# Loads of a three-layer attention kernel reordered around its first attentions, and one masked q moved to ScalarE

## The chip, the cores and the metric

The kernel runs on one core of one Trainium2 chip. The metric is device time in microseconds of the whole program. The core has five engines that run side by side, each with its own instruction stream in a fixed order: TensorE (PE in the profile; its weight loads are PEld), VectorE (DVE), ScalarE (ACT), GpSimd (POOL) and SyncE (SP). SP and ACT issue the transfers (DMAs) between memory and the on-chip SBUF; matmuls write to PSUM.

## The reference

There are 16 batches of 256 tokens with 256 features, a stream x and a context y. Three attentions and an MLP follow one another per batch, each attention with 16 heads of 16 features:

- layer 0: q from rmsnorm(x)·g_q, k and v from rmsnorm(y)·g_c; softmax over the unmasked keys; output projection, added to x, and another rmsnorm with g_out;
- layer 1: layernorm, causal self-attention with rotary position terms on q and k, biases, output projection, residual;
- layer 2: layernorm for q, k and v from y itself, rotary terms, no mask, output projection, residual;
- MLP: layernorm, 256 to 1024, tanh-gelu, 1024 to 256, residual.

All is float32. Layernorm's gain is folded into the weights in the kernel (w = g·w), and its bias into the projection biases (b·w, a product of a vector and a weight matrix).

## The kernel before, in words

`ORDER` (line 31) lists 48 attentions; digit i is the layer of attention i, and equal digits take the batches in turn. The first five are of layer 0, the first of layer 1 is i=5, the first of layer 2 is i=11. After them comes the MLP, two batches at a time.

One attention works in feature-major tiles. `q` and `k` (`by_feature`, L290) and `v` (`by_token`, L303) are projections of 16 matmuls into a PSUM tile d of 512 columns, of pool psD (three buffers). `scores(n)` computes block n of the score matrix, transposed, into two tiles S of 1024 columns (pool psS has two), and ScalarE takes each through exp into pt (L483). A causal attention has three blocks, with a GpSimd select (L490) that zeroes what lies above the diagonal; the others have four. `values(n)` multiplies pt with v into A (L511, one buffer in psA). A row of ones in v gives the sums of the softmax. `take` copies A to av and stores it to a scratch tensor hop in memory; `end` reads the sums and the rotated output oT back; `invert` takes the reciprocal and spreads it over another scratch trip; `divide` and `project` finish.

The masked q: heads are paired, and `qm` holds q twice, once with the odd heads zeroed and once with the even ones. For layers 1 and 2 `rotated` (L393) makes ScalarE add the bias, VectorE swap halves (a shuffle), multiply by the cosine and sine tables and add; then two VectorE operations (L424) write the two masked copies. k goes the same way without the masking.

The work is written out by hand in a loop over i and n (from line 879): block n of attention i stands beside q (n=0), k (n=1) and v (the last but one) of attention i+1, the output projection of i-2, and the statistics and norms of i+2. The order on every engine is the written one, and so is the order of the DMAs on SP's queue. There an entry waits for its data and holds up all that follow it; each of the DMAs also waits for an earlier one to land, since eight semaphores are used in turn.

Before the loop all starting loads are issued (L93 to L125): vec, the three weights of layer 0 and its output weight on ACT's queue, x, xT (x transposed), yT, y and the mask on SP's. For attention 0 `spread` brings the row scale of x across the partitions with a matmul against `ident`. For later ones of layer 0 `send` and `receive` do it through memory (rq).

Weights of later layers come inside the loop from SP's queue: sa (layer 1) before i=0, ca (layer 2) and fc1 at i=0, sao, cao and fc2 at i=1. `fold_bias` at i=1, n=3 forms the products b·w of sa, ca and fc1 on TensorE (L185), stores them to memory and reads them back transposed in the next entry of the queue (L196); `fold_cols` uses them at i=3. `fold_v` forms the one for v of layer 1. `fold_gain` (L226) is g·w. Two `idle` matmuls (L167) run before the first data.

Of the kernel before, what the change touches and what calls it, by code (L numbers as in the profile page):

```python
# [15 lines left out]
P = 128  # L16
# [29 lines left out]
def xattn_kernel(  # L46
# [45 lines left out]
    def load_x(b):  # L92
        nc.sync.dma_start(out=rows_of(b), in_=x[b].rearrange("(c p) d -> p c d", p=P))  # L93
        xTs[b] = work.tile([P, KC, S], F32, tag="xT", name=f"xT{b}", bufs=3)
        nc.sync.dma_start(out=xTs[b], in_=xt[b].rearrange("(k p) s -> p k s", p=P))

# [16 lines left out]

    vec = ctile([P, NVEC + 2], "vec")
    nc.scalar.dma_start(out=vec, in_=vecs)
    load_x(0)
    w0_sb = ctile([P, KC, 3 * D], "w0")
    load_w(w0_sb, w0, nc.scalar)
    load_y(0)
    mask_u8 = ctile([P, B * NC], "mask_u8", U8)  # L120
    nc.sync.dma_start(out=mask_u8, in_=mask)
    load(1)
    w0o_sb = ctile([P, KC, D], "w0o")
    load_w(w0o_sb, [w0_o], nc.scalar)
    load(2)  # L125
# [39 lines left out]
    idle = dense_ps()  # L165
    for n in range(2):
        nc.tensor.matmul(  # L167
            idle, lhsT=ident, rhs=zeros, start=True, stop=True
        )

# [4 lines left out]
    def fold_bias():  # L175

        ps = dense_ps()
        sets = (
            [(sa_sb, 0, V_B1), (sa_sb, D, V_B1), (ca_sb, 0, V_B2), (ca_sb, 0, V_B2)],
            [(fc1_sb, j * D, V_B3) for j in range(4)],  # L180
        )
        for n, items in enumerate(sets):
            for k in range(KC):
                for j, (w, at, vcol) in enumerate(items):
# [3 lines left out]
                        rhs=w[:, k, at : at + D],  # L188
# [3 lines left out]
        nc.scalar.copy(sb, ps)  # L192
        hop = dram.tile([4, 2 * D], F32, tag="fold", name="fold_hop", bufs=1)
        nc.sync.dma_start(out=hop, in_=sb[0:P:32])
        cols = ctile([P, 4, 2, KC], "cols")
# [6 lines left out]
    def fold_cols(cols):  # L202
        qk = vec[:, V_QK : V_QK + 8].rearrange("p (n t) -> p n t", t=KC)
        nc.vector.tensor_tensor(qk_bias[:, 0:3], cols[:, 0:3, 0], qk[:, 0:3], ALU.add)
        nc.vector.tensor_copy(qk_bias[:, 3], qk[:, 3])
# [18 lines left out]
    def fold_gain(w, cols, vcol, chunks=range(KC)):  # L224
        for k in chunks:
            nc.vector.tensor_scalar(  # L226
# [57 lines left out]
    def by_feature(src, w, at):  # L284

        ps = dense_ps()
        for t in range(KC):
# [23 lines left out]
    class Att:  # L311
# [36 lines left out]
        def spread(self):  # L348

            self.rq = work.tile([P, S], F32, tag="rq", name="rq")  # L350
            ps = dense_ps()
# [59 lines left out]
        def q(self):  # L411
# [11 lines left out]
            for i in range(2):  # L423
                nc.vector.tensor_scalar(self.qm[:, :, i, :], a, parity[i], None, ALU.mult)  # L424
# [437 lines left out]
    with tc.manual_schedule():  # L862
        do(0, "stats_x")
        fold_gain(w0_sb, slice(0, D), V_GQ)
        fold_gain(w0_sb, slice(D, 2 * D), V_GC)
        do(0, "turn", "spread", "q", "k", "stats_y")
# [12 lines left out]
        for i in range(N_ATT):  # L879
# [12 lines left out]
            for n in range(len(a.blocks)):  # L892
# [8 lines left out]
                if n == 0:  # L901
# [22 lines left out]
                    do(i + 1, "q")  # L924
# [31 lines left out]
                if i == 0 and n == 1:  # L956
                    load_w(ca_sb, ca, nc.sync)
                if i == 0 and n == 2:
                    load_w(fc1_sb, [fc1], nc.sync)
                if i == 1 and n == 0:  # L960
                    load_w(sao_sb, [sa_o], nc.sync)
                    load_w(cao_sb, [ca_o], nc.sync)
                if i == 1 and n == 2:
                    load_w(fc2_sb, [fc2], nc.sync)
# [504 lines left out]
```

## Time and profile before

| what | us |
|---|---|
| median of 3 runs (lowest, highest) | 946.64 (946.43, 946.78) |
| the profiled execution's own time | 946.89 |
| its span, first to last instruction | 945.2 |
| PE busy | 931.8 |
| DVE busy | 665.9 |
| ACT busy | 546.8 |
| POOL busy | 305.6 |
| mean granted TensorE clock, share of full | 0.997 |
| HBM read, written | 50.92 MB, 30.17 MB |

In lines of a profile the name before `<-` is what is written, the names after it what is read; x and a number count instructions; the last bracket gives the idle time before the group and what ended it. A line of the chain gives start, length and what ran. A line of a stretch gives its bounds and length, then busy time and instruction count of PE, PEld, DVE, ACT and POOL, then the granted clock, the DMA share and GB/s. DMAs are busiest in the first 26 us, at about 330 GB/s; over the span they move 86 GB/s.

### The profile page before, as it was taken

How to read it: one execution, taken by the hardware profiler on the slowest of the kernel's cores; microseconds unless marked ns; L12 is line 12 of the kernel's file. 1: busy time of each engine (PE TensorE's matmuls, PEld its weight loads, DVE VectorE, ACT ScalarE, POOL GpSimd, SP SyncE). 2: the span in 40 equal slices, each digit the busy share in tenths (PEclk: the TensorE clock that was granted, in tenths of full speed). 3: DMA queues.
4: the chain of work that ended last, by engine and by line, in shares of the span. 5: the costliest groups of instructions: out<-in, count | busy, mean ns of one | idle time of the engine just before them, and what ended most of it. 6: DMA issues, size and time to landing. Idle time of an engine off the chain costs nothing.

```text
span 945.2 us, 29295 instructions
## 1 busy us (share of the span) xinstructions
PE 931.8 (99%) x12374; PEld 549.6 (58%) x12374; DVE 665.9 (70%) x1438; ACT 546.8 (58%) x770; POOL 305.6 (32%) x501
## 2 busy tenths in 40 slices
PE   8999999999999999999999999999999999999997
PEld 3444555445454555455454454455444799999997
DVE  4346777787777787768876667998877576666663
ACT  3656656666666666756656666666666634444440
POOL 4122543324253464243343333454133021222200
PEclk9999999999999999999999999999999999999999
DMA  9543442323232233222343221222222100000001
GB/s 304 192 133 109 136 132 71 122 77 121 82 116 87 67 125 107 91 87 62 125 127 126 81 91 59 79 74 81 65 75 79 42 23 24 12 12 24 24 24 48
DMA packets 97955, 83.06 MB, mean 88 GB/s; under 512 B 21524, under 2 KB 97300, under 8 KB 97816
## 3 DMA queue, kind: packets, MB, share of 16 engines
q1 hardware_dynamic: 96584, 80.05, 26.7%
q8 instruction: 99, 1.62, 0.7%
q10 hardware_dynamic: 1232, 1.07, 0.3%
q14 instruction: 40, 0.33, 0.1%
HBM read 50.92 MB, written 30.17 MB: 86 GB/s over the span
## 4 chain that ended last, share of the span: by engine, by line
PE 95%; DMA 2%; DVE 1%; POOL 0%; ACT 0%; SPq 0%; issue 0%; ACTq 0%; DVEq 0%
PE S L472 19%; PE A L511 18%; PE d L303 17%; PE d L290 17%; PE upX L676 6%; PE A L774 5%; PE downZ L774 3%; PE upZ L676 3%; PE d L270 2%; PE d L774 2%; PE d L676 1%; PE d L652 1%; PE downX L774 1%; DMA w<-in_w_Wk 1%; DMA fold_hop<-fold 1%; DMA hop<-av 0%
## 5 line engine op out<-in xcount | busy, mean ns | idle before, releaser
L483 ACT ACTIVATE pt<-S 128x1024 f32<-128x1024 f32 x224 | 217.3, 1022 | 122.3 <-PE S L472 122.3
L472 PE MATMUL S<-qm,kT 32*128 32x512 f32 (+1 forms) x1536 | 201.9, 600 | 2.3 <-ACT hT L275 1.4
L511 PE MATMUL A<-pt,va 128*32 128x256 f32 (+1 forms) x3072 | 189.6, 368 | 2.3 <-DVE av L528 2.3
L511 PEld LDWEIGHTS A<-pt,va 128*32 128x32 f32 x3072 | 80.3, 109 | 156.0 <-issue 100.3
L483 ACT ACTIVATE pt<-S,sy 128x1024 f32<-128x1024 f32 x128 | 135.7, 1111 | 47.3 <-PE S L472 46.7
L490 POOL TENSOR_SCALAR_AFFINE_SELECT pt<-pt 128x512 f32<-128x512 f32 x128 | 89.5, 716 | 61.0 <-ACT pt L483 60.5
L472 PEld LDWEIGHTS S<-qm,kT 32*128 32x128 f32 x1536 | 62.1, 183 | 68.1 <-issue 39.9
L234 POOL TENSOR_SCALAR r_ln<-bmv 128x2 f32<-128x2 f32 x48 | 13.8, 287 | 222.5 <-DVE bmv L253 221.3
L279 POOL TENSOR_TENSOR cur<-cur,bias 128x512 f32<-128x512 f32 x48 | 66.7, 1395 | 56.5 <-DVE xn L259 56.5
L398 ACT ACTIVATE a<-d,qk_bias 128x256 f32<-128x256 f32 x128 | 53.8, 471 | 51.2 <-PE d L290 41.3
L290 PE MATMUL d<-hT,sa 128*32 128x256 f32 x1024 | 61.1, 379 | 0.0
L571 DVE TENSOR_TENSOR cur<-d,cur 128x512 f32<-128x512 f32 x32 | 22.0, 687 | 50.1 <-PE d L303 50.1
L406 DVE TENSOR_TENSOR u<-u,turn 128x512 f32<-128x512 f32 x64 | 53.9, 843 | 0.0
L528 DVE COPY av<-A 128x512 f32<-128x512 f32 x47 | 32.4, 689 | 26.9 <-PE A L511 26.9
L259 DVE TENSOR_SCALAR xn<-cur,bmv,r_ln 128x256 f32<-128x256 f32 x96 | 50.7, 577 | 0.8 <-POOL r_ln L235 0.3
L406 DVE TENSOR_TENSOR a<-a,turn 128x512 f32<-128x512 f32 x64 | 47.0, 735 | 2.2
L402 DVE STREAM_SHUFFLE u<-a 128x512 f32<-128x512 f32 x64 | 47.6, 743 | 0.0
L714 ACT ACTIVATE g<-g,fb 128x256 f32<-128x256 f32 x96 | 41.0, 499 | 11.1 <-DVE g L703 11.1
L290 PEld LDWEIGHTS d<-hT,sa 128*32 128x32 f32 x1024 | 33.2, 110 | 22.0
L234 POOL TENSOR_SCALAR r_o<-ms_o 128x2 f32<-128x2 f32 x16 | 4.7, 294 | 126.8 <-DVE sq L242 116.4
L562 DVE TENSOR_TENSOR oT<-oT,inv 128x512 f32<-128x512 f32 x48 | 42.7, 889 | 1.9 <-DMA inv<-inv_hop 1.9
L769 DVE TENSOR_TENSOR g<-g,g 128x512 f32<-128x512 f32 x64 | 40.9, 682 | 0.0
(149 smaller groups left out, 1560.7 us busy)
## 6 DMA issues: line engine op xcount, KB each, us to landing
hop<-av SPq DMA_DIRECT2D x96, 256.0 KB
oT<-hop SPq DMA_DIRECT2D x96, 128.0 KB
inv<-inv_hop SPq DMA_DIRECT2D x96, 128.0 KB
cur<-in_x SPq DMA_DIRECT2D x16, 256.0 KB
xT<-in_xt SPq DMA_DIRECT2D x16, 256.0 KB
yT<-in_yt SPq DMA_DIRECT2D x16, 256.0 KB
y<-in_y SPq DMA_DIRECT2D x16, 256.0 KB
out<-res SPq DMA_DIRECT2D x15, 256.0 KB
```

Of the source, the lines that this page charges most:

```text
L259: nc.vector.tensor_scalar(xn[:, c, :], src[:, c, :], mv[:, c, 0:1], r[:, c : c + 1], ALU.subtract, ALU.mult,)
L279: nc.gpsimd.tensor_tensor(t, t, bias_sb[:, row : row + D].unsqueeze(1).to_broadcast([P, NC, D]), ALU.add)
L290: nc.tensor.matmul(ps[j : j + 32, t * S : (t + 1) * S], lhsT=w[:, k, at + t * P + j : at + t * P + j + 32], rhs=src[:, k, :], start=(k == ...
L303: nc.tensor.matmul(ps[j : j + 32, c * D : (c + 1) * D], lhsT=src[:, k, c * P + j : c * P + j + 32], rhs=w[:, k, at : at + D], start=(k == ...
L398: nc.scalar.activation(a[:, t], ps[:, t], AF.Identity, bias=bias[:, t : t + 1])
L406: nc.vector.tensor_tensor(t, t, table.unsqueeze(1).to_broadcast([P, KC, S]), ALU.mult)
L472: nc.tensor.matmul(ps[:, j, 2 * m * u : 2 * m * (u + 1)] .rearrange("p (i s) -> p i s", i=2), lhsT=self.kT[r, t, kc * P : (kc + 1) * P], r ...
L483: nc.scalar.activation(pt[:, :, :w], ps[:, :, :w], AF.Exp, scale=scale)
L490: nc.gpsimd.affine_select(out=diag, in_=diag, compare_op=ALU.is_ge, fill=0.0, base=0, pattern=[[0, 2], [0, 2], [1, P]], channel_multiplier=-1,
L511: nc.tensor.matmul(self.av[32 * r : 32 * r + 32, i, q0:S], lhsT=self.va[:, kc, 8 * t + 2 * r + i, :], rhs=pts[r // 2][:, r % 2, i * m : (i ...
L676: nc.tensor.matmul(banks[c // 2][:, (c % 2) * S : (c % 2 + 1) * S], lhsT=a[:, c * P : (c + 1) * P], rhs=b, start=(first and c % 2 == 0), s ...
L774: nc.tensor.matmul(ps[:, c, :], lhsT=a[f // 2][:, f % 2, c * P : (c + 1) * P], rhs=b[:, f, :], start=(first and c == 0 and f == 0), stop=True,
```

## The change

- **Loads.** Only vec, Wq and Wk (on ACT) and xT, x, yT, y of batch 0 (on SP, xT now ahead of x) are issued first. The rest of the starting loads stand on SP behind a `gate`: a one-word store that reads Wq after its gain is folded in. Wv and Wo move from ACT's queue to SP's.
- **Later weights.** ca moves to i=3, cao and fc1 to i=4, fc2 to i=6.
- **Folds.** `fold_bias` is split: for sa at i=1 (8 matmuls, the two products twice over), for ca and fc1 at i=6 (16). The read-back is a function of its own, at i=2 and i=8. `fold_v` moves to i=0, n=3. The gain of fc1 goes from VectorE at i=6 and 10 to GpSimd at i=10 and 12, and the combining steps of the MLP's weights start after i=12 instead of i=10.
- **First attention.** q is computed before `spread`; k in two halves with a copy each; `stats_y` between; the masked q in four pieces. Wq's gain comes first on VectorE, ahead of the statistics of x. `spread` uses psA's tile, the idle matmuls psS's and are 512 and 256 wide.
- **Masked q.** Where attention i is causal and i+1 is of layer 1 or 2 (i = 21, 28, 38, 40, 42), the second masked copy is an ACTIVATE on ScalarE, written right after the q that it belongs to.

```diff
     def load_x(b):
-        nc.sync.dma_start(out=rows_of(b), in_=x[b].rearrange("(c p) d -> p c d", p=P))
         xTs[b] = work.tile([P, KC, S], F32, tag="xT", name=f"xT{b}", bufs=3)
         nc.sync.dma_start(out=xTs[b], in_=xt[b].rearrange("(k p) s -> p k s", p=P))
+        nc.sync.dma_start(out=rows_of(b), in_=x[b].rearrange("(c p) d -> p c d", p=P))
...
+    w0_sb = ctile([P, KC, 3 * D], "w0")
+    load_w(w0_sb[:, :, : 2 * D], w0[:2], nc.scalar)
     load_x(0)
-    w0_sb = ctile([P, KC, 3 * D], "w0")
-    load_w(w0_sb, w0, nc.scalar)
     load_y(0)
     mask_u8 = ctile([P, B * NC], "mask_u8", U8)
-    nc.sync.dma_start(out=mask_u8, in_=mask)
-    load(1)
     w0o_sb = ctile([P, KC, D], "w0o")
-    load_w(w0o_sb, [w0_o], nc.scalar)
-    load(2)
...
-    def fold_bias():
+    def fold_bias(sets):
...
-        nc.scalar.copy(sb, ps)
-        hop = dram.tile([4, 2 * D], F32, tag="fold", name="fold_hop", bufs=1)
-        nc.sync.dma_start(out=hop, in_=sb[0:P:32])
-        cols = ctile([P, 4, 2, KC], "cols")
+        nc.scalar.copy(sb[:, :w], ps[:, :w])
+        hop = dram.tile([4, w], F32, tag=f"fold{len(sets)}", name="fold_hop", bufs=1)
+        nc.sync.dma_start(out=hop, in_=sb[0:P:32, :w])
+        return hop
+
+    def fold_back(hop):
...
-    def q(self):
+    def q(self, shared=False):
...
-            for i in range(2):
-                nc.vector.tensor_scalar(self.qm[:, :, i, :], a, parity[i], None, ALU.mult)
+            nc.vector.tensor_scalar(self.qm[:, :, 0, :], a, parity[0], None, ALU.mult)
+            if shared:
+                nc.scalar.activation(self.qm[:, :, 1, :], a, AF.Copy, scale=parity[1])
+            else:
+                nc.vector.tensor_scalar(self.qm[:, :, 1, :], a, parity[1], None, ALU.mult)
+
+        def first_qk(self):
+            self.qm = work.tile([P, KC, 2, S], F32, tag="qm", name="qm", bufs=2)
+            self.kT = work.tile([P, KC, S], F32, tag="kT", name="kT", bufs=2)
+            ps = by_feature(self.hT, self.w, 0)
+            self.spread()
+            for t in range(KC):
+                nc.scalar.copy(self.kT[:, t], by_feature(self.kvT, self.w, D, [t])[:, t])
+            self.stats_y()
+            for t in range(KC):
+                for i in range(2):
+                    nc.vector.scalar_tensor_tensor(
+                        self.qm[:, t, i, :], ps[:, t], parity[i], self.rq, ALU.mult, ALU.mult
+                    )
...
+        idle = psS.tile([P, 2, 512], F32, tag="S", name="idle")[:, 0]
+        for n in (512, 256):
+            nc.tensor.matmul(idle[:, :n], lhsT=ident, rhs=zeros[:, :n], start=True, stop=True)
+        fold_gain(w0_sb, slice(0, D), V_GQ)
+
+        gate = dram.tile([1, 1], F32, tag="gate", name="gate", bufs=1)
+        nc.sync.dma_start(out=gate, in_=w0_sb[0:1, KC - 1, 0:1])
+        load_w(w0_sb[:, :, 2 * D :], w0[2:], nc.sync)
+        nc.sync.dma_start(out=mask_u8, in_=mask)
+        load(1)
+        load_w(w0o_sb, [w0_o], nc.sync)
+        load(2)
         do(0, "stats_x")
-        fold_gain(w0_sb, slice(0, D), V_GQ)
         fold_gain(w0_sb, slice(D, 2 * D), V_GC)
-        do(0, "turn", "spread", "q", "k", "stats_y")
+        do(0, "turn", "first_qk")
...
-                    do(i + 1, "q")
+                    if i + 1 < N_ATT:
+                        att(i + 1).q(shared=a.causal)
...
-                if i == 0 and n == 1:
-                    load_w(ca_sb, ca, nc.sync)
-                if i == 0 and n == 2:
-                    load_w(fc1_sb, [fc1], nc.sync)
+                if i == 0 and n == 3:
+                    fold_v()
                 if i == 1 and n == 0:
                     load_w(sao_sb, [sa_o], nc.sync)
-                    load_w(cao_sb, [ca_o], nc.sync)
                 if i == 1 and n == 2:
-                    load_w(fc2_sb, [fc2], nc.sync)
...
                 if i == 1 and n == 3:
-                    cols = fold_bias()
-                    fold_v()
+                    sa_hop = fold_bias([[(sa_sb, 0, V_B1), (sa_sb, D, V_B1)] * 2])
+                if i == 2 and n == 2:
+                    sa_cols = fold_back(sa_hop)
...
+                if i == 3 and n == 2:
+                    load_w(ca_sb, ca, nc.sync)
                 if i == 3 and n == 3:
-                    fold_cols(cols)
+                    fold_sa(sa_cols)
+                if i == 4 and n == 2:
+                    load_w(cao_sb, [ca_o], nc.sync)
+                    load_w(fc1_sb, [fc1], nc.sync)
+                if i == 6 and n == 2:
+                    load_w(fc2_sb, [fc2], nc.sync)
+                if i == 6 and n == 3:
+                    ca_hop = fold_bias(
+                        [[(ca_sb, 0, V_B2)] * 4, [(fc1_sb, j * D, V_B3) for j in range(4)]]
+                    )
+                if i == 8 and n == 2:
+                    ca_cols = fold_back(ca_hop)
                 if i == 8 and n == 3:
                     fold_gain(ca_sb, slice(0, D), V_G2)
-                if i in (6, 10) and n == 3:
-                    fold_gain(fc1_sb, slice(0, FF), V_G3, [i // 10])
-                if n == 1 and i > 10 and not a.causal:
+                    fold_ca_fc1(ca_cols)
+                if i in (10, 12) and n == 1:
+                    fold_gain(fc1_sb, slice(0, FF), V_G3, [i // 12], nc.gpsimd)
+                if n == 1 and i > 12 and not a.causal:
```

More of the change, by code (lines that the diff above doesn't have):

```diff
@@ L163, in xattn_kernel @@
     nc.gpsimd.memset(zeros, 0.0)
[L165 to L169, printed above, removed]
     qk_bias = ctile([P, 4, KC], "qk_bias")
     fb1 = ctile([P, FF // P], "fb1")
-    def fold_bias():
+    def fold_bias(sets):
         ps = dense_ps()
[L178 to L181, printed above, removed]
+        w = len(sets) * D
         for n, items in enumerate(sets):
             for k in range(KC):
-                for j, (w, at, vcol) in enumerate(items):
+                for j, (t, at, vcol) in enumerate(items):
                     nc.tensor.matmul(
@@ L187, in fold_bias @@
                         lhsT=vec[:, vcol + k : vcol + k + 1].to_broadcast([P, 32]),
-                        rhs=w[:, k, at : at + D],
+                        rhs=t[:, k, at : at + D],
                         start=(k == 0), stop=(k == KC - 1), skip_group_check=True,
@@ L191, in fold_bias @@
         sb = work.tile([P, 2 * D], F32, tag="a", name="fold")
-        nc.scalar.copy(sb, ps)
-        hop = dram.tile([4, 2 * D], F32, tag="fold", name="fold_hop", bufs=1)
-        nc.sync.dma_start(out=hop, in_=sb[0:P:32])
-        cols = ctile([P, 4, 2, KC], "cols")
+        nc.scalar.copy(sb[:, :w], ps[:, :w])
[3 more added lines that the diff above has]
+    def fold_back(hop):
+        w = hop.shape[1]
+        cols = ctile([P, 4, w // D, KC], f"cols{w // D}")
         nc.sync.dma_start(
@@ L200, in fold_bias, with fold_sa, fold_ca_fc1 @@
         return cols
[L202 to L205, printed above, removed]
+    qk_cols = vec[:, V_QK : V_QK + 8].rearrange("p (n t) -> p n t", t=KC)
+    def fold_sa(cols):
+        nc.vector.tensor_tensor(qk_bias[:, 0:2], cols[:, 0:2, 0], qk_cols[:, 0:2], ALU.add)
+    def fold_ca_fc1(cols):
+        nc.vector.tensor_tensor(qk_bias[:, 2], cols[:, 0, 0], qk_cols[:, 2], ALU.add)
+        nc.vector.tensor_copy(qk_bias[:, 3], qk_cols[:, 3])
         nc.vector.tensor_tensor(
@@ L222, in fold_v, with fold_gain @@
         nc.vector.tensor_tensor(row, ps[:, :D], row, ALU.add)
-    def fold_gain(w, cols, vcol, chunks=range(KC)):
+    def fold_gain(w, cols, vcol, chunks=range(KC), eng=nc.vector):
         for k in chunks:
-            nc.vector.tensor_scalar(
+            eng.tensor_scalar(
                 w[:, k, cols], w[:, k, cols], vec[:, vcol + k : vcol + k + 1], None, ALU.mult
@@ L281, in add_bias, with by_feature @@
         )
-    def by_feature(src, w, at):
+    def by_feature(src, w, at, ts=range(KC)):
         ps = dense_ps()
-        for t in range(KC):
+        for t in ts:
             for k in range(KC):
@@ L350, in spread @@
             self.rq = work.tile([P, S], F32, tag="rq", name="rq")
-            ps = dense_ps()
+            ps = psA.tile([P, 2, S], F32, tag="A", name="A").rearrange("p i s -> p (i s)")
             for c in range(NC):
```

## The prediction

> **What bounds the kernel now.** A score step is one block's S matmuls (L472) to the next block's. I read the busy totals first, then the chain of work that ended last between 22 and 72 us, a table of stretches, and the timeline where TensorE (PE) is not fed.
>
> ```profile
> PE 931.8 (99%) x12374; PEld 549.6 (58%) x12374; DVE 665.9 (70%) x1438; ACT 546.8 (58%) x770; POOL 305.6 (32%) x501
> ```
>
> PE is the bound: time goes away only where PE idles, runs at a lowered clock, or has fewer matmuls. Its idle places: the start, 64 to 67 us, two gaps of 0.69 us at 345 and 449, and the last store. The chain names the second:
>
> ```profile
> 49.70 6.40 DMA fold_hop<-fold
> ...
> 56.57 3.55 DMA hop<-av
> ...
> 60.14 1.94 DMA sums<-hop
> ...
> 66.96 1.93 PE A L511 x16
> ```
>
> The SyncE (SP) queue is in order. The read-back of the bias fold (L196) sits in it behind its own write, so hop, sums, and with them VectorE (DVE), come late; the copy of av that frees A (L528) ends at 66.8.
>
> ```profile
> 64.00:67.00 3.00, 0.69 (x12) 0.07 (x6) 2.92 (x9) 2.12 (x2) 1.46 (x2) 0.92 0.15 48
> 67.00:71.00 4.00, 4.00 (x48) 2.04 (x48) 3.26 (x9) 0.00 (x0) 1.86 (x4) 0.64 0.70 224
> ```
>
> PE does 0.69 of 3 us, then runs at clock 0.64. Scores start at 63.51 and next at 71.12, against the usual 3.80 (32.26, 36.06, 39.86): 3.81 us lost.
>
> ```profile
> 8.51 0.62 DVE L226 TENSOR_SCALAR w<-w,vec 128x256 f32<-128x256 f32 x2 [2.60 <-DMA w<-in_w_Wk]
> 11.60 1.14 PE L472 MATMUL S<-qm,kT 32*128 32x512 f32 x8 [0.69 <-ACT kT L433]
> 15.17 0.64 PE L354 MATMUL d<-ident,pad 128*32 128x128 f32 x16 [0.57 <-POOL pad L235]
> 27.47 2.13 PE L472 MATMUL S<-qm,kT 32*128 32x512 f32 x8 [0.26 <-ACT pt L483]
> 589.18 1.95 ACT L483 ACTIVATE pt<-S 128x1024 f32<-128x1024 f32 x2 [0.26 <-PE S L472]
> 591.51 1.01 DVE L422 TENSOR_TENSOR a<-a,u 128x512 f32<-128x512 f32 x1
> 596.36 1.01 DVE L431 TENSOR_TENSOR kT<-a,u 128x512 f32<-128x512 f32 x1
> 597.51 1.14 PE L472 MATMUL S<-qm,kT 32*128 32x512 f32 x8
> 345.75 1.14 PE L472 MATMUL S<-qm,kT 32*128 32x512 f32 x8 [0.69 <-ACT hT L275]
> ```
>
> The start waits for Wk (8.5). In the causal attention of 588 the next k is ready at 597.4, 0.1 before its scores: no slack. At 345 the same chain is 0.69 late.
>
> [...] the trace's 2.31 us gap already gave 0.64[...] Here every ACT row does follow the order written. [...] the rotary multiply takes 0.69 us alone and 1.12 beside a select. [...]
>
> **The change part by part.**
>
> Start. Ahead of the gate stand six loads of 256 KB and vec, 1.6 MB. At the trace's 330 GB/s from 2.0 us they end near 7, so Wk comes at 7.0 to 7.5. But first_qk changes what ends last. DVE scales Wq first (Wq came at 5.2, two by 0.35, to 5.9), and only then takes the sums of squares of x (1.0, to 6.9); POOL's pad (1.15) is ready at 8.1; spread on PE 0.65, ACT's rq 0.4: 9.2. PE is in order: q, spread, k half 0, k half 1 (0.87 each): 10.5. On DVE the Wk gain (0.62) and stats_y (1.0) fit before 9.2, two qm pieces by about 0.4 give 10.0. So scores start at 10.5 instead of 11.60: -1.1 (bounds -0.6, -1.6). The wait for the second pad (0.57 at 15.17) shrinks with it: DVE finishes qm at 10.9, Wv gain 11.5, cast, x(1) 12.7, pad 13.8; spread at 13.9 against 15.17: another -0.2.
> The gate itself is a one-word store; SP behind it waits until 5.9. Behind it queue Wv (issued 6.5, needed 11.5), mask, load(1), w0o, load(2). Their issue was already held by earlier landings (L99 waited until 8.50 for Wk), and load(1)'s y landed at 13.66; now about 12. Later loads slip by the DMA gap, about 0.8 us: bias and turn, which drained at 26.3, come near 27. DVE's add in fold_v waits for that; next behind it on DVE is the av copy, needed near 29. Hidden.
>
> Fold matmuls. Before: 16 + 8 instructions between scores at 39.86 and 44.52, 24 by 0.108 = 2.6 plus drain, 2.91 in all. After: fold_v at i=0 (8), the sa fold at i=1 (8), the ca and fc1 fold at i=6 (16). With 8, a scores-to-scores step is 1.07 + 0.67 + 1.19 = 2.93. At i=0 the step was 29.53 - 26.14 = 3.39 from values to values, 1.66 of it a wait for ACT's exp, which fold_v now fills: -0.45. At i=1, 4.66 becomes 2.93: -1.73. At i=6, +1.73. Sum -0.45.
>
> SP stall. The read-back now stands at i=2, n=2, a step or more after its write; ca comes at i=3, cao and fc1 at i=4, fc2 at i=6, each two score steps before the next hop (7.6 us against at most 2.4 MB, 7 us). The 3.81 us go; bounds -2.3 (the idle alone) and -3.8.
>
> Masked q on ScalarE. It is shared only where the running attention is causal and the next is not layer 0: i = 21, 28, 38, 40, 42, five times. DVE loses one of two operations of 0.76 (0.44 without POOL). But on ACT the copy stands between q's bias ACTIVATEs and the next two exps, and waits for DVE's add. At i=38, from the scores at 587.95: bias ends +1.0, DVE's shuffle 0.74 and three operations by 0.69 (POOL has nothing to select now) end +3.8; copy to +4.5 (0.7). The exps, at +1.2 before, run +4.5 to +6.4; then k's bias ACTIVATEs +6.4 to +7.2 (were +3.9 to +4.8). Queued behind: POOL's selects, then values at +7.1 (was +6.6), project, turn: PE is ready for the next scores at +10.1 (was +9.56). DVE's chain for k starts at +7.25: 2.8 us if alone, +10.1; if it meets the selects, now pushed beside it, 3.4, +10.7. So the scores come 0.6 to 1.2 late, I take 0.9; at 21 and 28, where 0.69 is lost already, -0.1 to +0.5, I take 0.25. Sum 3 x 0.9 + 2 x 0.25 = +3.2 (bounds +1.6, +4.6).
>
> The rest at nothing: the fc1 gain moves to POOL at i=10 and 12 (1024 wide, at most two by 1.74 of L627's), into idle stretches of about 9 us before the next r_o; without that cover up to 3 us twice. The combine steps start two attentions later and still end long before the MLP. 2 x 512 idle columns become 768, before the first load lands. x and xT swap, inside the start.
>
> Sum: -1.3 - 0.45 - 3.81 + 3.2 = -2.4. The profiled execution took 946.89 (span 945.2, 1.7 around it), the median is 946.64; the step applies to both: **944.3 us**. A difference under 0.2%, 1.9 us, is about what a measurement here cannot tell from none.
>
> **The rivals.**
> The copy is hidden: if exps have room, the five cost nothing and the two gaps of 0.69 go: -5.6 - 1.4 = -7, 939.7. For it: ACT is busy 58%, less in causal attentions. Against: k's chain ends 0.1 us before its scores.
> Contention: kT at the late bound, +4.6, and fold_v waiting for sa, which lands near 24 if everything slips (needed 25.4), +0.5: -0.5, 946.1, no change.
> The stall stays: if hop or sums are late for other reasons, DVE is still blocked near 62: -1.3 - 0.45 + 3.2 = +1.4, 948.1, also near no change. For it: hop to sums took 6.7 us at 31.39; against: ca and fc1 filled the DMAs then, and are gone.
> Slower: the held exps. It decides from (5.55 + 1.9)/5 = 1.5 us a time. The price would be met if DVE reaches q's add later, each 1 us of delay before it holding exp, select, values and k alike: at 1.8 us, +9 - 5.6 = +3.4, 950.1. Against: in all five places DVE had sat idle 0.23 to 0.67 us when q's bias released it, so nothing is queued ahead of that chain.
>
> **How the numbers follow.** Forecast 0.38 (its own range 942 to 944.7); hidden copy 0.16; contention 0.22; stall stays 0.10; slower 0.14. Faster 0.54, same 0.32, slower 0.14. The range for 8 in 10 runs from near the hidden copy, 940.3, to 947.8, leaving out half of the slower case and a little below.
>
> **What would show it.** First scores near 10.5 and no PE gap or lowered clock between 55 and 70; the fold's read-back without its 6 us wait; fold matmuls at three places; in the five causal attentions exp starting 3 us later behind the copy and the next scores 0.6 to 1.2 late. Wrong if those exps are not held, if PE waits for fold_v's operands near 25, or if idle PE lowers the clock there or in the start.

## The result and the profile after

The changed kernel takes 954.37 us in the median (953.02 to 957.98, six executions) beside 946.71 for the kernel before on the same chip: ratio 1.0079, 95% interval 1.0058 to 1.0101. The forecast was 944.3, the range 940.3 to 947.8. The profiled execution took 953.12 us, its span is 951.4 against 945.2.

First the busy totals of the changed kernel, then three of TensorE's waits in it (engine and line, what ended the wait: us in total, times, longest), two of the kernel before, and three stretches of the changed kernel: the two where the kernel before had stood still (0.69 of 3 us busy) and run at a granted clock of 0.64, and a new one.

```profile
PE 936.0 (98%) x12390; PEld 551.9 (58%) x12390; DVE 663.8 (70%) x1434; ACT 548.8 (58%) x777; POOL 306.9 (32%) x503
```

```profile
PE d L267 <- DVE xn L256: 3.0, 2, 2.3
PE S L488 <- DVE kT L447: 2.9, 5, 0.6
...
PE A L527 <- DVE av L544: 1.0, 1, 1.0
```

```profile
PE A L511 <- DVE av L528: 2.3, 1, 2.3
...
PE S L472 <- ACT hT L275: 1.4, 2, 0.7
```

```profile
64.00:67.00 3.00, 3.00 (x48) 1.31 (x44) 1.04 (x4) 1.91 (x4) 0.54 (x3) 1.00 0.12 15
67.00:71.00 4.00, 4.00 (x68) 1.89 (x62) 1.56 (x5) 2.79 (x5) 0.00 (x0) 1.00 0.28 88
100.75:103.00 2.25, 0.10 (x4) 0.00 (x0) 0.81 (x4) 0.31 (x1) 0.54 (x1) 1.00 0.19 47
```

The old hole is gone: PE is busy in every microsecond from 64 to 71. The kernel before waited once for av, in that hole, and twice 0.7 us for hT. The changed kernel waits for xn (two places, 2.3 and 0.7), for kT (the five places of the masked q) and for av in another place.

To see what each is worth, take the start of every score step (attention i, step n) in both profiles and subtract. The difference changes in a few places only, and between them it is constant to some hundredths:

| at (i, n) | what | difference changes by, us | prediction |
|---|---|---|---|
| (0, 1) | start | -1.34 | -1.3 |
| (1, 0) to (2, 1) | fold_v moved, sa fold alone | -1.27 | -2.18 |
| (3, 2) | stall at 64 us | -3.81 | -3.81 |
| (6, 0) | wait for xn | +2.33 | 0 |
| (7, 0) | ca and fc1 fold | +1.73 | +1.73 |
| (8, 0) | wait for xn | +0.81 | 0 |
| (9, 2) | wait for av | +1.06 | 0 |
| 22, 29 | masked q on ScalarE | +0.85, +0.86 | +0.25 each |
| 39, 41, 43 | masked q on ScalarE | +1.53, +1.54, +1.52 | +0.9 each |
| after (47, 0) | MLP part | +0.4 | 0 |

The sum is +5.8 at (47, 0) and +6.2 in the span. The last +0.4 belongs to this one execution: from (47, 0) on the other kernels with the same MLP part take 225.5 to 225.8 us, the kernel before 225.5, this profile 225.9. All that was expected to be gained was gained but for 0.9 us of the folds, in this execution; then 4.2 us were lost in attentions 5 to 9 and 6.3 in the five places of the masked q.

The first loss, from the profile of SyncE's queue (start, length, what was issued), in the changed kernel and then, around the same hop, in the kernel before:

```profile
87.69 0.38 SPq L545 DMA_DIRECT2D hop<-av  x1
88.12 0.46 SPq L111 DMA_DIRECT2D cao<-in_ca_wo  x1
88.64 0.49 SPq L111 DMA_DIRECT2D fc<-in_fc  x1
89.17 0.52 SPq L94 DMA_DIRECT2D xT<-in_xt  x1
...
93.62 0.89 SPq L545 DMA_DIRECT2D hop<-av  x1
100.20 0.55 SPq L552 DMA_DIRECT2D sums<-hop  x1
```

```profile
97.96 0.37 SPq L529 DMA_DIRECT2D hop<-av  x1
102.24 0.55 SPq L536 DMA_DIRECT2D sums<-hop  x1
```

cao and fc1 (1.25 MB) are written for step 2 of attention 4, which starts at 80.48. SyncE comes to them at 88.1, when attention 5 has begun, and right behind them stands the 1 MB of inputs for a later attention. The second half of the hop goes out at 93.62 and has landed at 100.20, when the read of the sums can go: 6.6 us, against 4.3 in the kernel before. Then the chain runs through VectorE (start, length, what ran):

```profile
100.20 1.93 DMA sums<-hop
102.13 0.02 issue
102.15 0.19 DVE sums L563
102.34 0.02 issue
102.37 0.35 DVE sums L564
102.72 0.24 DVE xn L256
```

VectorE had waited 7.5 us for the sums, and xn, which TensorE turns next, is queued behind them. At (8, 0) it is fc2 in place of fc1 (the hop takes 6.11 us), and ahead of (9, 2) VectorE waits 0.87 us for the read-back of the second fold, which takes 5.55 us for 8 KB in single words; the copy of av that frees A stands behind it. From the same chain:

```profile
124.79 6.11 DMA hop<-av
130.97 1.96 DMA sums<-hop
...
148.37 5.55 DMA cols<-fold_hop
```

The second loss, in the order of time around the q of attention 39 (i=38), in the changed kernel. The scores before it started at 589.17; in the kernel before, all this stood against 587.95.

```profile
593.07 0.73 ACT L422 ACTIVATE qm<-a,vec 128x512 f32<-128x512 f32 x1 [2.92 <-DVE a L419]
...
593.70 1.91 ACT L499 ACTIVATE pt<-S 128x1024 f32<-128x1024 f32 x2
...
594.75 2.04 PE L488 MATMUL S<-qm,kT 32*128 32x512 f32 x8
...
595.51 0.83 ACT L395 ACTIVATE a<-d,qk_bias 128x256 f32<-128x256 f32 x2
...
597.17 0.87 DVE L403 TENSOR_TENSOR a<-a,turn 128x512 f32<-128x512 f32 x1
597.96 1.12 DVE L403 TENSOR_TENSOR u<-u,turn 128x512 f32<-128x512 f32 x1
...
599.12 1.01 DVE L447 TENSOR_TENSOR kT<-a,u 128x512 f32<-128x512 f32 x1
...
600.27 1.14 PE L488 MATMUL S<-qm,kT 32*128 32x512 f32 x8 [0.58 <-DVE kT L447]
```

ScalarE waits 2.92 us for VectorE's add, copies, and only then runs the two exps, +4.5 after the scores instead of +1.2. The next scores (594.75) take 2.04 instead of 1.14: their second tile S has to wait until a held exp has emptied it (its weight loads wait 0.61 us for that exp). k's bias follows at +6.3, and VectorE's chain for k now runs beside GpSimd's pushed-back selects (595.68 to 599.58): its multiplies and its add take 0.87, 1.12 and 1.01 us, where those for q at 590.96, with no select beside them, took 0.69, 0.68 and 0.69. From shuffle to the end of kT it is 3.75 us. The scores of attention 39 start 0.90 + 0.58 = 1.48 late.

### The profile page after: what moved, and what is told of

Read it like the earlier page. It is cut to its first block, busy times and chain, and to the rows that moved or that the text cites. A ratio compares the mean times of both kernels' runs of the same rounds, so it can differ in the third digit from the quotient of the medians.

```text
span 951.4 us, 29306 instructions
## 1 busy us (share of the span) xinstructions
PE 936.0 (98%) x12390; PEld 551.9 (58%) x12390; DVE 663.8 (70%) x1434; ACT 548.8 (58%) x777; POOL 306.9 (32%) x503
## 4 chain that ended last, share of the span: by engine, by line
PE 88%; DVE 5%; DMA 3%; ACT 2%; issue 1%; SPq 1%; POOL 0%; ACTq 0%; DVEq 0%
PE S L488 18%; PE A L527 17%; PE d L287 15%; PE d L300 14%; PE upX L692 6%; PE A L790 5%; PE upZ L692 3%; PE downZ L790 3%; PE d L267 2%; PE d L790 2%; PE d L692 1%; ACT pt L499 1%; DVE u L399 1%; DVE u L403 1%; ACT a L395 1%; DVE a L403 1%
## 5 line engine op out<-in xcount | busy, mean ns | idle before, releaser
L488 PE MATMUL S<-qm,kT 32*128 32x512 f32 (+1 forms) x1536 | 206.3, 600 | 2.9 <-DVE kT L447 2.9
L506 POOL TENSOR_SCALAR_AFFINE_SELECT pt<-pt 128x512 f32<-128x512 f32 x128 | 86.4, 693 | 70.0 <-ACT pt L499 69.7
L256 DVE TENSOR_SCALAR xn<-cur,bmv,r_ln 128x256 f32<-128x256 f32 x96 | 53.5, 606 | 0.8 <-POOL r_ln L232 0.3
L403 DVE TENSOR_TENSOR u<-u,turn 128x512 f32<-128x512 f32 x64 | 51.8, 810 | 0.0
```

What stands on the lines that cost most here:

```text
L403: nc.vector.tensor_tensor(t, t, table.unsqueeze(1).to_broadcast([P, KC, S]), ALU.mult)
L488: nc.tensor.matmul(ps[:, j, 2 * m * u : 2 * m * (u + 1)] .rearrange("p (i s) -> p i s", i=2), lhsT=self.kT[r, t, kc * P : (kc + 1) * P], r ...
L506: nc.gpsimd.affine_select(out=diag, in_=diag, compare_op=ALU.is_ge, fill=0.0, base=0, pattern=[[0, 2], [0, 2], [1, P]], channel_multiplier=-1,
```

## The experiments

Times are medians, beside the median of the kernel before on the same chip; "steps" are starts of score steps as above. The kernel before read 946.71 to 947.72 on the chips used, so medians of two experiments that ran beside different medians of it can be compared to about 1 us only.

**No shared copy.** The changed kernel with both masked copies on VectorE.

```diff
-                        att(i + 1).q(shared=a.causal)
+                        att(i + 1).q()
```

> The changed kernel with both masked copies of q on VectorE again in all five places, the rest as changed. Theory (the copy holds the exps in ScalarE's queue): the five losses seen between score steps, 0.79 + 0.79 + 1.48 + 1.47 + 1.48 = 6.0 us, all go; the profiled 953.1 becomes 947.1, and the two gaps of 0.69 us near 345 and 449 are there again as before the change. Rival (the later exps are harmless and the loss is from something else in those places, such as GpSimd beside VectorE): less than 2 us goes, 951 or more, and the score step after q stays longer than the 4.03 us it had.

Measured: 948.36 (before 947.12, ratio 1.0014, 1.0003 to 1.0024), profiled 945.24. In the steps the five places give back 0.82, 0.85 and three times 1.54, 6.3 in all, and TensorE's two waits of 0.7 for hT are back. The median is 6.0 below the changed kernel's. The profile is 1.9 lower than expected: 0.3 more in the five places, 0.5 less lost at (6, 0) and nothing at (8, 0), 0.4 in the MLP part. The theory holds.

**The copy later.** The same ScalarE copy, written behind k's bias.

```diff
+        def q_rest(self):
+            if self.layer > 0 and self.rest is not None:
+                nc.scalar.activation(self.qm[:, :, 1, :], self.rest, AF.Copy, scale=parity[1])
...
                     do(i + 1, "k")
+                    if i + 1 < N_ATT:
+                        att(i + 1).q_rest()
```

> The changed kernel with the same ScalarE copy written behind k's bias in ScalarE's queue, where ScalarE idles 1.98 us, instead of right behind q's. Theory (place in the queue, not the work): exps start where they did, +1.2 us after their scores, nothing of the 6.0 us is lost, and VectorE, freed of one operation of 0.76 us, has k ready that much earlier, so the two gaps of 0.69 us shrink or go: 953.1 - 6.0 - 1.4 = 945.7, at worst 947.1. Rival (the work itself on ScalarE, or GpSimd's selects beside VectorE, costs): 950 or more, with the scores still 0.6 us or more late.

Measured: 947.64 (before 947.12, ratio 1.0003, 0.9991 to 1.0015), profiled 947.07. The five places give back 1.6 each, 8.0 in all, 1.7 more than with no copy on ScalarE: the two old gaps of 0.69 are gone too. The order of time around attention 38 shows it, scores here at 588.01:

```profile
589.25 1.94 ACT L502 ACTIVATE pt<-S 128x1024 f32<-128x1024 f32 x2 [0.26 <-PE S L491]
...
591.95 0.84 ACT L395 ACTIVATE a<-d,qk_bias 128x256 f32<-128x256 f32 x2 [0.76 <-PE d L287]
...
592.68 0.72 ACT L427 ACTIVATE qm<-a,vec 128x512 f32<-128x512 f32 x1
...
595.62 0.69 DVE L450 TENSOR_TENSOR kT<-a,u 128x512 f32<-128x512 f32 x1
```

The exps run at +1.2 again, the copy takes the same 0.72 us in time that ScalarE idled before, and kT ends at +8.3 where it ended at +9.4. So the work on ScalarE was never the cost; its place was. In this profile, however, 1.9 us are lost around (6, 0) over what the changed kernel lost there, and a table of stretches says why:

```profile
101.50:104.20 2.70, 0.25 (x8) 0.00 (x0) 0.87 (x4) 0.46 (x1) 0.64 (x1) 1.00 0.23 57
104.20:108.00 3.80, 3.75 (x36) 1.90 (x40) 2.59 (x8) 2.13 (x3) 0.96 (x2) 0.67 0.27 83
```

Here the wait for xn is 2.5 us, and the 3.8 us behind it ran at a clock of 0.67. In the changed kernel's profile a wait of 2.25 left the clock at 1.00.

**The copy alone.** The kernel before with the copy as the change places it (the same edit of `q`, and `shared=a.causal`).

> The kernel before with the ScalarE copy alone, placed as in the change. Theory: the loss is independent of the start and the loads: 946.7 + 6.0 = 952.7, with the next scores 1.48 us late in three places and 0.79 in two. By the prediction's own term: +3.2, 949.9. Rival (the loss needs the later loads or the shifted start): within 1 us of 946.7.

Measured: 954.46 (before 947.12, ratio 1.0081, 1.0064 to 1.0097), profiled 952.62. The steps show 0.80, 0.81 and three times 1.48 at once, 6.3 with what follows in the next steps. The loss needs nothing else of the change.

**The loads elsewhere.** The changed kernel with the later weights where no load of inputs follows.

```diff
-                if i == 4 and n == 2:
-                    load_w(cao_sb, [ca_o], nc.sync)
+                if i == 4 and n == 0:
                     load_w(fc1_sb, [fc1], nc.sync)
-                if i == 6 and n == 2:
+                if i == 10 and n == 0:
+                    load_w(cao_sb, [ca_o], nc.sync)
+                if i == 12 and n == 0:
                     load_w(fc2_sb, [fc2], nc.sync)
```

> The changed kernel with the later weights loaded where no load of inputs follows before a hop: fc1 in the first step of attention 4, ahead of VectorE's inverse in SyncE's queue, cao in the first step of attention 10, fc2 in that of attention 12. Theory (2 MB and 1 MB behind each other hold the hop of av for 6.6 and 6.1 us): the hop takes about 4.3 us again, the 2.33 us lost before the scores of attention 6 and the 0.81 before those of 8 go: 953.1 - 3.1 = 950.0, and the spread between executions shrinks if it is TensorE's gap of 2.25 us that lowers the clock in some of them. Rival (the wait of 2.25 us comes from VectorE's own order, or from a read that is late anyway): less than 1 us goes, 952 or more, and VectorE still waits over 5 us for the sums.

Measured: 951.03 (before 947.12, ratio 1.0054, 1.0034 to 1.0075), profiled 948.76. The steps give back 2.33, 0.81, and also the 1.06 at (9, 2), 4.2 in all: the second read-back lands 4.4 us after its issue here instead of 5.55, and VectorE waits 0.24 for it instead of 0.87. SyncE's queue:

```profile
80.50 0.45 SPq L111 DMA_DIRECT2D fc<-in_fc  x1
...
91.70 0.37 SPq L545 DMA_DIRECT2D hop<-av  x1
97.23 0.55 SPq L552 DMA_DIRECT2D sums<-hop  x1
```

The hop is issued 1.9 us earlier and takes 5.5 instead of 6.6; my 4.3 was wrong, for with the 1 MB of inputs alone ahead of it the hop still takes 5.5 here, and that is soon enough. The loss sets in somewhere between: counting from the start of attention 5's scores, sums were asked for after 7.7 us in the kernel before and 9.0 here (no loss), after 11.2 in two kernels below (1.44 and 1.64 lost) and after 12.1 in the changed kernel (2.33). The spread between executions did not shrink (948.8 to 954.6), so that part of the expectation failed.

**The second read-back used later.** The changed kernel with the sums into qk_bias and fb1 one attention on.

```diff
                     fold_gain(ca_sb, slice(0, D), V_G2)
+                if i == 9 and n == 2:
                     fold_ca_fc1(ca_cols)
```

> The changed kernel with only the use of the second read-back later: the sums into qk_bias and fb1 in step 2 of attention 9 instead of step 3 of attention 8. Theory (VectorE waits 0.87 us for the 4-byte read-back, issued one step ahead, and the copy of av behind it frees A late): the loss of 1.06 before step 2 of attention 9 goes, 953.1 - 1.1 = 952.0. Rival (the copy of av is late for the order of VectorE's other work): the 6.59 us of that step stay, against 5.53 before.

Measured, in one execution: 953.57. The step to (9, 2) is 5.53 again, the 1.06 is gone: shown. The total does not show it: in this execution the wait before (6, 0) was 2.43 us long, 0.43 more was lost there than in the changed kernel's profile, and the next stretch of 3.5 us had a clock of 0.67, another 1.28.

**The loads from ScalarE's queue.** cao and fc1 in the same step, from the other queue.

```diff
-                    load_w(cao_sb, [ca_o], nc.sync)
-                    load_w(fc1_sb, [fc1], nc.sync)
+                    load_w(cao_sb, [ca_o], nc.scalar)
+                    load_w(fc1_sb, [fc1], nc.scalar)
```

> The changed kernel with the loads of cao and fc1, 1.25 MB, issued in the same step of attention 4 by ScalarE's DMA queue instead of SyncE's. Theory A (the hop of av is late because it stands behind 2.25 MB in one queue's order): it now stands behind the 1 MB of inputs alone, takes 4.3 to 5.5 us instead of 6.6, and the loss before attention 6 falls from 2.33 to under 1. Theory B[...]: the hop still takes 6 us or more and the loss stays at 1.7 to 2.4.

Measured, in one execution: 952.77, with 1.44 lost at (6, 0), between the two expectations. ScalarE issued the loads at 84.16 and 87.13, up to four microseconds ahead of where SyncE did, so the position changed as well as the queue, and SyncE's own issues behind it were held up nearly 2 us (yT at 92.89). The hop took 5.40. What the other queue alone is worth is not shown, for the position moved with it. In this run's chain a read on SyncE's own queue, rq<-rq_hop, issued at 88.67 just after fc1 on the other one, took 6.49 us, and the hop went out when it had landed.

**The read-back alone.** The kernel before, with the read-back of the fold at i=2, n=2, where the change has it.

```diff
-                    cols = fold_bias()
+                    back = fold_bias()
                     fold_v()
+                if i == 2 and n == 2:
+                    cols = fold_back(back)
```

> The kernel before with the fold's read-back alone moved, from right behind its write to step 2 of attention 2. Theory (SyncE held by that wait is the whole of the 3.81 us stall near 64 us): 947.1 - 3.8 = 943.3, and the score step of attention 3 is 3.80 everywhere. Rival (hop and sums are late there for the loads of fc2 and rope that go ahead of them): at most the half of it goes, 945.2 or more, with VectorE still waiting for sums near 62.

Measured: 947.73 (before 947.35, ratio 1.0002, 0.9994 to 1.0011). The step of attention 3 loses its stall (3.64 of it), and the next attention gains it: +4.02 at (4, 0) and +2.26 at (4, 1). The waits between 60 and 90 us, and a line of its chain:

```profile
DVE sums L550 <- DMA sums<-hop: 8.9, 1, 8.9
...
PE d L273 <- DVE xn L262: 3.5, 1, 3.5
```

```profile
70.29 4.73 DMA hop<-av
```

So the place of the read-back does clear this stall, but the loss comes back one attention later and the total is unchanged. SyncE gets to the read-back at 64.73 here, against 58.76 in the kernel below that has the late loads as well: the order of write and read-back was a link in the chain, not what made SyncE late.

**The late loads alone, and both.** The kernel before with cao and fc2 loaded in attentions 10 and 12, the read-back still right behind its write; then the same with the read-back moved.

```diff
-                    load_w(cao_sb, [ca_o], nc.sync)
...
-                    load_w(fc2_sb, [fc2], nc.sync)
...
+                if i == 10 and n == 0:
+                    load_w(cao_sb, [ca_o], nc.sync)
+                if i == 12 and n == 0:
+                    load_w(fc2_sb, [fc2], nc.sync)
```

> The kernel before with cao loaded in attention 10 and fc2 in 12, all else as before, the fold's read-back still right behind its write. Theory (the stall at 64 us needs the 1 MB of fc2 ahead of the fold's write; the read-back then waits 6.4 us for a write that would take about 2): the stall of 3.81 us goes or falls below 1, 943.3 to 944. Rival (the order of read-back behind write is enough): at least 3 us of it stays, 946 or more.

> The kernel before with both: read-back moved to step 2 of attention 2, and cao and fc2 loaded late. If the late loads alone take the stall away, this equals them, or is worse where the 4-byte read-back (5 us) stands ahead of the next load of inputs and hop, as it stalled attention 4 when moved alone. If both are needed, this takes 3.8 away, 943.3, and neither alone does.

Measured: 942.69 (before 947.42, ratio 0.9952, 0.9937 to 0.9968) and 942.84 (ratio 0.9953, 0.9938 to 0.9968). Behind the start, which varies, each has exactly -3.81 at (3, 2) and no other change over 0.12. With the loads out of the way the place of the read-back made no difference. In the first, SyncE's queue and the stretches where the hole was:

```profile
48.61 0.54 SPq L194 DMA_DIRECT2D fold_hop<-fold  x1
50.76 0.35 SPq L196 DMA_DIRECT2D cols<-fold_hop  x1
```

```profile
64.00:67.00 3.00, 3.00 (x56) 1.54 (x52) 2.69 (x6) 2.12 (x2) 1.85 (x4) 1.00 0.95 247
67.00:71.00 4.00, 4.00 (x60) 1.97 (x64) 0.00 (x0) 3.18 (x4) 0.00 (x0) 1.00 0.50 166
```

The write that took 6.40 us behind 1 MB of fc2 takes 2.1 without it. Its wait was what the chain named; the loads in front were the cause. fc2 stood 2.65 us ahead of the write and the 256 KB of cao 9.1 us; these runs move both and do not separate them.

**Three repairs together.** The changed kernel with the late copy, the loads elsewhere and the later use.

> The changed kernel with three repairs together: the ScalarE copy behind k's bias, fc1 loaded in the first step of attention 4, cao in that of 10 and fc2 in that of 12, and the sums of the ca and fc1 biases (qk_bias, fb1) taken in step 2 of attention 9 instead of step 3 of attention 8. Theory (the changed kernel loses in these places alone): its profiled 953.1 less 7.8 (the five copies and the two old gaps, as measured with the copy behind k), less 4.2 (2.33 + 0.81 + 1.06) gives 941.1, some 6 us under the kernel before, in the profiled execution. Rival (the median of the changed kernel's executions stands over its profile for another reason, such as its start): the profile shows 941 but the median lies 1.5 to 3 us above it, as it did with the repairs taken singly. Rival (the repairs meet each other): 944 or more in the profile.

Measured: 942.12 (before 947.35, ratio 0.9939, 0.9925 to 0.9952), 12 us below the changed kernel. Profiled 942.78, against 941.1 expected, with 1.64 still lost before (6, 0): fc1 had been issued at 81.31, and the read of inv went out 4.1 us after the write of inv_hop instead of 1.6 as in the kernel before, which held up SyncE.

**fc1 by quarters.** That kernel, with fc1 in four pieces.

```diff
-                if i == 4 and n == 0:
-                    load_w(fc1_sb, [fc1], nc.sync)
+                if i in (2, 3, 4, 5) and n == 0:
+                    c = slice((i - 2) * D, (i - 1) * D)
+                    load_w(fc1_sb[:, :, c], [fc1[:, c]], nc.sync)
```

> The kernel with the three repairs, and fc1 loaded by quarters of 256 KB in the first steps of attentions 2, 3, 4 and 5 instead of 1 MB at once in that of 4. In the profile of the three repairs 1.64 us is still lost before the scores of attention 6, and SyncE's read of inv waits 2.6 us behind fc1. Theory (1 MB in the engines[...] puts SyncE, and so the next loads and hops, late): a quarter delays them by under 1 us, the 1.64 us go, profile near 939.5. Rival (hop and sums are late there for the 1 MB of inputs alone, as they are before the change): the step before attention 6 stays over 5 us, profile 941.

Measured: 941.71 (before 947.42, ratio 0.9939, 0.9925 to 0.9952). The step to (6, 0) is 3.96, as in the kernel before: the 1.64 are gone. The profile fell by 0.7 only, for its start came 0.9 later than in the last one (second step at 17.73 instead of 16.82). The median fell by 0.4; whether the start is the reason there too is not shown.

**The start alone, and its idle matmuls.** The kernel before with the new start; then the same with

```diff
-        for n in (512, 256):
+        for n in (512, 512):
```

> The kernel before with the new start alone (first loads, gate, halves of k, place of the Wq gain), the fold, the later loads and q as before. Prediction's term: scores of the first attention from 11.60 to 10.5, second step 1.3 us earlier; seen in the changed kernel 1.34 to 1.53 in one execution. Theory (the start gains what the profile showed): 947.2 - 1.3 = 945.9. Rival (the first landings vary by more than that from one execution to the next, so that the gain is not in the median): within 0.5 us of the kernel before.

> The kernel before with the new start alone, as in the run before, but two idle matmuls of 512 columns as before the change, instead of 512 and 256. Theory (the shortened idle matmuls leave TensorE cold: the first 32 matmuls of q took 1.93 to 3.64 us in eleven profiles of the new start and 1.9 in every one of the old): they take 1.9 us now, scores start at 10.1 to 10.5 instead of 11.88, and the second step at 16.0 to 16.3: 0.8 to 1.4 better than with the old start, 1 to 2 better in the median than the new start with its own idle columns. Rival (the landings of the first loads alone scatter the start): the first matmuls still take over 2.3 us or the scores start at 11 or later, median as without it.

Measured: 948.60 (before 947.42, ratio 1.0010, 1.0001 to 1.0019) and 949.01 (before 947.72, ratio 1.0018, 1.0008 to 1.0029). The start alone gains nothing. The first matmuls of q, from the order of time: the changed kernel, the new start alone, and that with the full idle columns.

```profile
5.49 2.06 PE L287 MATMUL d<-xT,w 128*32 128x256 f32 x32 [0.48 <-DVE w L223]
```

```profile
5.80 3.64 PE L281 MATMUL d<-xT,w 128*32 128x256 f32 x32 [0.79 <-DVE w L217]
```

```profile
5.80 1.93 PE L281 MATMUL d<-xT,w 128*32 128x256 f32 x32
```

The same 32 matmuls take 1.93 to 3.64 us. Each trace holds records of the granted clock (start, length, share), and the first of them, of full clock, explains the scatter:

| profile | matmuls start | first clock record | they took | 1.91 + half the time before the record |
|---|---|---|---|---|
| kernel before | 6.47 | 5.06 | 1.91 | 1.91 |
| changed kernel | 5.49 | 5.80 | 2.06 | 2.07 |
| no shared copy | 5.39 | 6.82 | 2.61 | 2.63 |
| second read-back used later | 5.62 | 7.84 | 3.00 | 3.02 |
| repaired change, full idle columns (below) | 5.83 | 7.18 | 2.58 | 2.59 |
| new start alone | 5.80 | 10.01 | 3.64 | all of it before the record |

The other twelve fit to 0.03 us, or took 3.64 wholly ahead of the record. So TensorE ran these matmuls at about half rate until that record began. The gap in front of the matmuls does not decide it: the 2.58 had none. With 512 and 256 idle columns the record begins at 5.35 to 11.60 (at 10.01 or later in three profiles of nine; the expectation counted eleven), with two of 512 at 5.06 to 7.18 in nine. So with the shortened idle matmuls TensorE was still slow for all of q in some executions (3.64 us in three profiles of nine, against none of the nine with full columns), and that was one reason. A start that reaches q at 5.4 to 5.9 also comes near or ahead of that record more often than the old one, which reaches q at 6.41 to 6.90 and was behind it in all six profiles.

But with 1.93 the scores started at 10.48, and the median was no better: at (3, 2) that execution lost 1.87 more than the kernel before. Behind the gate SyncE's queue runs later, though the scores run earlier: it came to ca at 28.67 instead of 27.39, and the hop of the first attention behind ca and fc1, loaded early as before the change, went out at 32.57 instead of 31.39 and took 7.6 us instead of 6.7.

**The best of both.** The kernel before with late loads and the late copy; and the same with the new start and two idle matmuls of 512.

> The kernel before with cao and fc2 loaded in attentions 10 and 12, and the ScalarE copy of q in the five places written behind k's bias; start, fold and read-back as before. Late loads alone gave 942.7; the copy behind k takes the two gaps of 0.69 us and about 0.1 in each of the other places: 942.7 - 1.7 = 941.0. Rival (what remains of the gain of the changed kernel, its start and its fold, is needed for 941): 942 or more.

> The same as the last with the new start and two idle matmuls of 512 columns. If the start gains once TensorE is warm: 941.0 - 1.0 = 940.0, and executions that agree within 1 us. If the start's gain does not show in the median even so: 941 or more.

Measured: 941.06 (940.71 to 941.46; before 947.72, ratio 0.9931, 0.9917 to 0.9945) and 942.35 (ratio 0.9945, 0.9931 to 0.9958). The first is the fastest kernel here, 13.3 us below the changed one, and has no gap of TensorE over 0.7 us between the start and the last store:

```profile
PE 930.6 (99%) x12374; PEld 549.0 (58%) x12374; DVE 660.9 (70%) x1433; ACT 549.9 (59%) x775; POOL 304.3 (32%) x501
```

In the second the second step comes 0.8 earlier and the stall at 64 us is back (TensorE waits 2.7 us for av), with fc2 gone. Its chain:

```profile
33.25 8.61 DMA hop<-av
...
54.16 5.28 DMA hop<-av
```

ca and fc1 stand ahead of that first hop.

**The repaired change with full idle matmuls.** fc1 by quarters, and 512 twice.

> The changed kernel with the three repairs and fc1 by quarters, and two idle matmuls of 512 columns instead of 512 and 256. With the later loads out of the way of attentions 2 and 3, the new start's earlier scores should not meet them: the first 32 matmuls take 1.9 us, scores start near 10.5 and the second step near 16.4, against 12.63 and 17.73 without the idle columns, no stall before step 2 of attention 3; the profile falls from 940.3 to near 939.0 and the median from 941.7 to near 940.5, below the 941.06 of the old start with late loads and the copy behind k. Rival (the start gives nothing to the median in any surrounding): 941.5 or more.

Measured: 941.46 (before 946.91, ratio 0.9942, 0.9928 to 0.9955). No stall at (3, 2), scores at 10.89, second step at 17.02 instead of 16.4. It is not below the 941.06 of the old start, though that kernel differs in the folds and in fc1 too, ran on another chip, and the intervals of the two ratios overlap. Where the start alone was exchanged (the kernel before, and the best of both), the median was no better with the new one.

## Why the prediction was wrong

**Start, -1.3.** Right in the changed kernel's profile (scores at 10.07, second step 1.34 earlier), but that was luck. Over the nine profiles with the change's idle columns the second step starts at 16.07 to 17.73, in the mean 16.8; with the old start at 16.96 to 17.47, in the mean 17.2. The step "2 x 512 idle columns become 768, before the first load lands", put at nothing, was wrong: in three of the nine the 32 matmuls behind them took 3.64 us instead of 1.9. It is not the whole of it, for with full idle columns the mean of three is 16.7. The loads behind the gate, which the working called hidden, were so in the changed kernel, but not in the kernels that have the new start and still load ca and fc1 early.

**Folds, -0.45; measured +0.46.** fold_v at i=0 filled TensorE's wait for exp, but in both kernels the second S tile behind it waits for the same exp, and the values after it start 12.06 us after step (0, 1) either way: 0 instead of -0.45. At i=1 the shortened step ran into ScalarE: S took 1.60 instead of 1.14, waiting for an exp, so -1.27 instead of -1.73. Where two exps take 2.12 us, a short step cannot be priced by matmuls alone. At i=6, +1.73 was right.

**SP stall, -3.81.** The size was right to a hundredth, the reason half right. The working read off the chain that the read-back "sits in it behind its own write". Moved alone, the read-back cleared this place (3.64) and cost 6.28 in the next attention; with cao and fc2 moved and the read-back left, all of it was gained. The change moved both, so the number came out.

**The later loads, at nothing.** This step failed: "each two score steps before the next hop (7.6 us against at most 2.4 MB, 7 us)". It set bandwidth against a distance in the program. SyncE reached the entry 7.6 us after its step had begun, behind its own waits, and then the weights, 1 MB of inputs and the hop followed each other without a gap. Cost: +2.33 and +0.81, and at (9, 2) +1.06 from a read-back used one step after its issue, which the working did not cost at all; either the later use or the loads elsewhere took that away.

**Masked q, +3.2; measured +6.3.** The mechanism came as described: exps at +4.5 to +6.4 and k's bias from +6.3, to a tenth; the 0.7 us for the copy was the author's estimate, and it took 0.73. Two terms were mis-sized. "PE is ready for the next scores at +10.1" was +10.5, because the block of scores before them (at 594.75 above) takes 0.90 longer, waiting for the S tile of a held exp, which the working left out; and k's chain took 3.75 us, not 2.8 to 3.4, so kT ended at +11.0, not +10.1 to +10.7. At 21 and 28, where 0.69 was lost already, this leaves 0.8, not 0.25.

The terms that were off are 0.9 (folds), 3.1 and 1.1 (loads, read-back) and 3.1 (masked q): 8.2, from -2.4 to the +5.8 of the profiles at (47, 0). The medians are 7.7 apart, the profiled executions 6.2: the changed kernel's profile is one of its fastest executions, and where the others lose more is not shown. Of the rivals, "the held exps" named the larger loss, but from VectorE being late, which it was not, and at a threshold of 1.5 us a time that was not met (6.3/5 = 1.26); the loads took it over. "Copy is hidden" would have been true one place further down ScalarE's queue. "The stall stays" was false where it looked, and true of attentions 5 and 7.

## What to carry to other kernels

- An operation handed to an engine with time to spare costs by its place in that engine's queue: put it behind the work that others wait for, at a point where its operands are long ready. The same copy was worth +6.3 us in one place and -1.7 in another.
- When a chain shows a transfer that takes three times its usual time (here 6.40 us against 2.1), look at what was issued ahead of it before moving the transfer. Spread large loads over idle stretches of the queue as it really runs, not of the program as written, and away from the next large load and the round trips behind it. Here fc1 in quarters instead of 1 MB at once took away the last 1.64 us.
- Price a shortened stretch of the busiest engine against the other engines' time for the same stretch (here 2.12 us of two exps), and measure a start over several executions (here its second step came at 16.07 to 17.73).

## What was not expected of the hardware

**Idle TensorE and its clock.** In nine profiles TensorE waits 1.99 to 4.30 us somewhere between the start and the last store. In eight of them (1.99, 2.31, 2.43, twice 2.50, 2.67, 3.49 and 4.30) the trace's clock records then read 0.50 for 3.41 us, for 6.83 at the wait of 3.49; in the changed kernel's profile, with 2.25, they do not, nor at waits of 1.07 to 1.71. In the four profiles where the score steps show the price (kernel before, late copy, read-back used later, read-back alone), the lowered clock cost 1.3 to 2.3 us more than the wait. So nearly equal waits fell either way, 2.25 at the full clock and 2.31 at half of it, and one of 1.99 was enough. What decides between them is not shown.

**Spread.** The kernels with late loads and the old start, free of such a gap, agree within 0.8 us from one execution to the next (942.47 to 943.19, 940.71 to 941.46); the changed kernel spread over 5 us, and with the late copy it spread over 8.5 (942.5 to 951.0). Only one execution of each kernel has a profile, but the mean granted clock is on record for all: of the twenty with the late copy, six read 0.996 and took 949.2 to 951.0 us, three read 0.999 or 1.000 and took 942.5 to 944.6. Of the changed kernel's six, 957.98 read 0.995, the two at 955.4 read 0.997 and the three at 953.0 to 953.3 read 0.998 to 1.000. So long executions and a lowered clock go together there; how much of the time is the clock and how much the waits ahead of it is not shown. The changed kernel with its loads elsewhere, which had no wait over 0.6 us behind the start, took 948.8 and 951.1 at 1.000 and 954.6 at 0.998; its spread of 5.8 stays open.

**A first burst at half speed.** Ahead of a trace's first clock record the table of stretches prints 1.00, while the same 32 matmuls took up to 3.64 us there and 1.9 behind it. A full clock in that column says nothing about the time before the first record.
